# Two-layer cross-attention on one core: the first contexts and queries transposed by TensorE and split from PSUM, key weights' low halves made by GpSimd, TensorE's first work in a fixed order

## The chip, the cores and the metric

One core of a Trainium2 chip. The core has five engines with their own instruction queues: TensorE (PE; its weight loads are listed apart as PEld), VectorE (DVE), ScalarE (ACT), GpSimd (POOL) and SyncE (SP), which here issues nearly all DMAs. Each queue runs in order; engines wait for one another on semaphores. The metric is the device time of one execution in microseconds, the median of several runs.

## The reference, cut to what matters

Two cross-attention layers in float32, batch 8, 100 query rows and 722 context rows of width 512. Layer 0 normalises queries and context with the same gain and bias, has 16 heads of 32, and is followed by a feed-forward block of width 2048; layer 1 attends to the raw context with 16 heads of 64.

```python
qn = _layer_norm(query, ln1_g, ln1_b)
kn = _layer_norm(key, ln1_g, ln1_b)
vn = _layer_norm(value, ln1_g, ln1_b)
Q = (qn @ wq + bq).reshape(B, Sq, H, HD)
K = (kn @ wk + bk).reshape(B, Sk, H, HD)
V = (vn @ wv + bv).reshape(B, Sk, H, HD)
scores = jnp.einsum('bqhd,bkhd->bhqk', Q, K) / jnp.sqrt(jnp.float32(HD))
attn = jax.nn.softmax(scores, axis=-1)
out = jnp.einsum('bhqk,bkhd->bqhd', attn, V).reshape(B, Sq, E)
out = out @ wo + bo
x = residual + out
y = _layer_norm(x, ln2_g, ln2_b)
y = jax.nn.gelu(y @ w1 + b1, approximate=False)
y = y @ w2 + b2
```

## The kernel before, in words

All large products are made in float16 with each operand split in two halves: the high half is the value rounded to float16, the low half what the rounding left. A product is three terms (`TERMS`, line 23): high by high, high by low weight, low by high weight. Weights are scaled by a power of two first, and the layer-0 gain is folded into the weights, its bias into a bias column per output (`bias_mm`, lines 261 to 267: matmuls of the raw float32 weights with one column, 4 per group of 128 outputs).

The program runs through 24 units: 8 of layer 0 (one per batch element, 16 heads each) and 16 of layer 1 (half of the heads of one batch element each). While one unit's heads are worked through, the projections of the next unit, weight preparation and feed-forward pieces are put between the heads; from line 1368 on a scheduler decides the order within each engine by its own estimate of times. Tiles come from pools with a fixed number of buffers, and an instruction waits for the buffer that it needs.

Lines 1257 to 1367 are the opening, in which no attention can run yet. There the kernel lists engines in `nc.in_order`; for those the order of the program text is kept. Before the change these are DVE, ACT, POOL and SP, but not PE.

The opening does this. The eight first inputs are loaded (`first_load`): six chunks of up to 128 rows of context 0 and the queries of batch elements 0 and 1. Each gets statistics (`first_stats`, `first_aggr`) and is normalised in place on DVE (`first_apply`). `first_high` rounds it to float16 on ACT, `first_low` makes the low half on GpSimd and sends both through a DMA transpose, issued by SP, into `ctxT[0, 0]` or `xT[0]`, where the contraction index lies on the partitions. The chunks go in two groups: 0 to 2, then 3 to 7.

Beside this each of the weights wk, wq and wv goes through a fixed series: load (`load0`), sum of squares on ACT (`square_of`), a column sum on PE and a short chain on DVE that gives the scale (`scale_steps`), high halves on ACT (`high0`), low halves on DVE (`low0`, lines 330 to 334), and the bias columns (`bias_mm`, `bias_of`). `biasp` has one PSUM tile for each name: those of k and q from the pool `ps_s` that later holds the scores, that of v from `ps_o`.

Then the first keys are projected: `k0[:2]` are the two halves (361 of 722 columns each) of the first 128 key outputs. Each half is one call of `piece` in `proj_k` (lines 645 to 666): 12 matmuls, the eviction on ACT and DVE to `KN`, and after the second half a store to DRAM (`KD`) and three loads back (`ks`), which put four heads in their place. `first_queries` does the same for the queries through `QD` and `QS`. The first scores (`S`) need both. `load0("o", wo)` and three small columns are loaded after the first group of context 1 has been prepared (`prep0(1)`, lines 1362 to 1367); `wo_block` works on them during the first heads.

Of the kernel before, what the change touches and what calls it, by code (L numbers as in the profile page):

```python
# [54 lines left out]
def xattn_kernel(  # L55
# [38 lines left out]
    def clear_padding0():  # L94
        for t in NM:
            nc.gpsimd.memset(t, 0.0)
        for t in PT:
            nc.gpsimd.memset(t[:, :, SQ:128], 0.0)
        for t in KSR:
            nc.gpsimd.memset(t[:, :, SK:], 0.0)  # L100
            nc.sync.dma_start(out=t[96:98, :, :SK], in_=MSD.rearrange("p (a b) -> p a b", a=4)[:, :, :SK])
# [23 lines left out]
    def psum(shape=(128, 512)):  # L125
        mis["n"] += 1
        if mis["pp"] and mis["n"] % 3 == 0:
            return NZB
        return ps_p.tile(list(shape), F32, tag="pp", name="pp")
# [123 lines left out]
    def load0(name, w, parts=1):  # L253
        raw0[name] = sp.tile([128, KC, E], F32, tag="raw", name=f"raw_{name}", bufs=3)
        for k in range(parts):
            sl = slice(KC // parts * k, KC // parts * (k + 1))
            nc.sync.dma_start(out=raw0[name][:, sl], in_=w.rearrange("(c p) n -> p c n", p=128)[:, sl])
# [1 line left out]
    biasp = {}  # L259

    def bias_mm(name, *ocs):
        if name not in biasp:
            if name == "v":
                biasp[name] = ps_o.tile([128, 512], F32, tag="O", name="bv")[:, :KC]
            else:
                biasp[name] = ps_s.tile([128, 2, 512], F32, tag="S", name="bS")[:, 0, :KC]
        bias_part(biasp[name], raw0[name], b1lc, ocs)

    def bias_of(name, bc, a=0, e=KC):
# [33 lines left out]
    def square_of(name):  # L303
        u = squares[name]
        for k in range(2 if name == "k" else 1):
            sl = slice(2 * k, 2 * k + 2) if name == "k" else slice(0, KC)
            nc.scalar.activation(
                WRES[name][:, 0, sl].rearrange("p c n -> p (c n)"), raw0[name][:, sl].rearrange("p c n -> p (c n)"),
                AF.Square, scale=gbm, accum_out=u[:, 5 * k : 5 * k + 1])
# [3 lines left out]
    def scale_steps(i, name):  # L313

        us = colsum(squares[name], 6)
        ut = small(1, tag="us")
        s = scale0[name] = const.tile([128, 1], F32, name=f"s_{name}")
        gs = gains[name] = const.tile([128, KC], F32, name=f"g_{name}")
        l = [lambda: nc.vector.tensor_reduce(ut, us, AX.X, ALU.add)] + pow2_steps(s, inv0[:, i : i + 1], ut, 0, 1)
        l.insert(5, lambda: nc.vector.tensor_scalar(gs, g1c, s, 1.0 / XS, ALU.mult, ALU.mult))  # L320
        return l
# [3 lines left out]
    def high0(name):  # L325
        w = w0[name] = WRES[name]
        for kc in range(KC):
            nc.scalar.activation(w[:, 0, kc, :], raw0[name][:, kc, :], AF.Copy, scale=gains[name][:, kc : kc + 1])

    def low0(name):  # L330
        w = w0[name]
        for kc in range(KC):
            nc.vector.scalar_tensor_tensor(
                w[:, 1, kc, :], raw0[name][:, kc, :], gains[name][:, kc : kc + 1], w[:, 0, kc, :], ALU.mult, ALU.subtract)

    def split_piece(dst_hi, dst_lo, raw, s, on_pool=False):
        nc.scalar.activation(dst_hi, raw, AF.Copy, scale=s)
# [35 lines left out]
    def hlt():  # L373
        return ring("hl", HL)
# [78 lines left out]
    def first_aggr(c):  # L453
        n = first_in[c][1]
        nc.vector.bn_aggr(mv8[:n, c, :], sts[c][:n])
# [2 lines left out]
        t, n = first_in[c]  # L458
        eng.tensor_scalar(t[:n], t[:n], mv8[:n, c, 0:1], r[:n], ALU.subtract, ALU.mult)

    hls = {}

    def first_high(c, eng):
        t, n = first_in[c]
        h = hls[c] = WRES["v", 0].rearrange("p t (a c) n -> p (t a) (c n)", a=2)[:, c] if c < 4 else hlt()
        (eng.copy if eng is nc.scalar else eng.tensor_copy)(h[:n, :E], t[:n])

    def first_low(c, eng):
        t, n = first_in[c]
        h = hls[c]  # L470
        eng.tensor_tensor(h[:n, E:], t[:n], h[:n, :E], ALU.subtract)
        if c < NCH:
            m = (n + 15) // 16 * 16
            to = ctxT[0, 0][:, :, c * 128 : c * 128 + m]
        else:
            m, to = SQP, xT[0][:, :, (c - NCH) * SQP : (c - NCH + 1) * SQP]
        nc.sync.dma_start_transpose(to, h[:m])

    def first_ucol():
        m2 = small(6, tag="m2")  # L480
# [159 lines left out]

    def proj_k(u):
        L, b, hf = unit_of(u)
        kn = {}

        def piece(oc, j):
            w = w0["k"] if L == 0 else w1res["k", hf]
            T = ctxT[L, b]
            if j == 0:
                kn[oc] = pool.tile([128, 2, SK], F16, tag="KN", name="KN", bufs=2)
            K = kn[oc]  # L650
            ps = psum()
            sl = slice(j * HALF, (j + 1) * HALF)
            for i, (a, w_) in enumerate(TERMS):
                for kc in range(KC):
                    nc.tensor.matmul(
                        out=ps[:, :HALF], lhsT=w[:, w_, kc, oc * 128 : (oc + 1) * 128], rhs=T[:, a * KC + kc, sl],
                        start=(i == 0 and kc == 0), stop=(i == 2 and kc == KC - 1))
            if L == 0:
                bias = bscaled["k"][:, oc : oc + 1]
                nc.scalar.activation(K[:, 0, sl], ps[:, :HALF], AF.Identity, bias=bias)  # L660
                nc.vector.scalar_tensor_tensor(K[:, 1, sl], ps[:, :HALF], bias, K[:, 0, sl], ALU.add, ALU.subtract)
            else:
                nc.scalar.copy(K[:, 0, sl], ps[:, :HALF])
                nc.vector.tensor_tensor(K[:, 1, sl], ps[:, :HALF], K[:, 0, sl], ALU.subtract)
            if j == 1:
                stack(oc)

        def stack(oc):
            K = kn[oc]
            if L == 0:  # L670
                KSt[u, oc] = KS = keys_tile(u, 4 * oc + 3)
                KD = dram.tile([128, 2, SK], F16, tag="KD", name="KD", bufs=4)
                nc.sync.dma_start(out=KD, in_=K)
                src = KD.rearrange("(h d) t k -> d h t k", d=32)
                for r in range(3):
                    nc.sync.dma_start(out=KS[32 * r : 32 * r + 32, :, :SK], in_=src[:, :, r % 2, :])
            else:
                if oc % 2 == 0:
                    KSt[u, oc // 2] = keys_tile(u, 2 * oc + 3)
                KS = KSt[u, oc // 2]  # L680
                for j in range(2):
                    for t in range(2):
                        nc.sync.dma_start(
                            out=KS[64 * t : 64 * t + 64, 2 * (oc % 2) + j, :SK], in_=K[64 * j : 64 * j + 64, t, :])
            if u > 0 and oc == (1 if u == LAST else 2 if u < B else 3):
                load_q(u)
        def item(oc, j):
            f = lambda: piece(oc, j)
            if j == 1 and (L == 0 or oc % 2 == 0):
                f.ready = keys_free  # L690
            return 2.0, f
        return [item(oc, j) for oc in range(4) for j in range(2)]
# [574 lines left out]
    def calls(l):  # L1267
        for f in l:
            f()
# [27 lines left out]
    square_bias("k", bkc)  # L1297
    zip_(A[:6], G_[5:])
    square_of("k")
    bias_mm("k", 0)  # L1300
    K = scale_steps(1, "k")
    calls(A[6:])
    for c in range(3):
        first_apply(c, ra[:, c : c + 1], V)
    for c in range(3):
        first_high(c, S_)
    clear_padding0()
    for c in range(3):
        first_low(c, P_)
    calls(K)  # L1310
    bias_mm("k", 1, 2, 3)
    high0("k")
    load0("v", wv)
    load_early(1, range(4))
    first_stats(3)
# [8 lines left out]
    first_stats(7)  # L1324
    first_aggr(6)
    first_aggr(7)
    Q = scale_steps(0, "q")
    bias_mm("q", 0)
    zip_(Bs, [none] * 3 + Q)
    for c in range(3, 6):  # L1330
        first_apply(c, rb[:, c - 3 : c - 2], V)
        first_high(c, S_)
        first_low(c, P_)
    high0("q")
    for c in range(6, 8):
        first_apply(c, rb[:, c - 3 : c - 2], V)
        first_high(c, S_)
        first_low(c, P_)
    low0("k")
    bias_of("k", bkc)  # L1340
    run(k0[:1])
    low0("q")
    square_bias("v", bvc)
    square_of("v")
    nc.vector.tensor_tensor(sig0, inv0[:, 0:1], inv0[:, 1:2], ALU.mult)
    nc.vector.tensor_scalar(sig0, sig0, 32.0 ** -0.5 * XS / XSQ, None, ALU.mult)
    bias_mm("q", 1)
    bias_of("q", bqc, 0, 2)
    run(k0[1:2])
    first_queries(0)  # L1350
    vs = scale_steps(2, "v")
    bias_mm("q", 2, 3)
    calls(vs)
    high0("v")
    low0("v")
    first_ucol()
    bias_of("q", bqc, 2, 4)
    bias_mm("v", 0, 1, 2, 3)
    nc.in_order = ("sync",)
    bias_of("v", bvc)  # L1360
    nc.in_order = ("vector", "sync")
# [194 lines left out]
```

## Time and profile before

| | us |
|---|---|
| median of 3 runs | 1536.39 (1535.56 to 1539.84) |
| the profiled execution, its time | 1540.27 |
| its span, first to last instruction | 1538.5 |
| busy: PE, DVE, ACT, POOL | 1385.8, 1015.8, 813.6, 580.4 |
| mean granted TensorE clock | 0.966 |

Layer 0 fills the program to about 650 us, layer 1 the rest. A row of the timeline has the start, the length from the first to the last of the merged instructions, the engine, a source line, the operation, output <- inputs, and the number of instructions; in brackets stands the idle time before and what ended it. All instructions pass through one helper, so the source line is 40 for nearly all, and the tiles' names tell them apart: `bS` and `bv` are bias columns, `nzb` the small sums, `pp` the projections. A float32 matmul shows as two rows. The time of a granted clock below 1.00 in a stage is the throttle's, not the kernel's choice.

### The profile page before, as it was taken

What the parts mean: (1) busy time and instruction counts of PE and PEld (TensorE: products, weight loads), DVE (VectorE), ACT (ScalarE), POOL (GpSimd) and SP (SyncE); (2) the same over time, 40 slices, a digit from 0 to 9 for tenths busy, and PEclk for the clock granted to TensorE, in tenths of its full rate; (3) what the DMA queues carried; (4) which work ended last, traced back from release to release, by engine and by line L of the source; (5) the groups of instructions that cost most, each with busy time, mean ns of one, the idle gap of its engine ahead of it and who ended that gap; (6) DMA issues with size and microseconds to landing.
All of it is one profiled execution on the core that took longest, in us unless ns stands there. A gap on an engine that the chain in (4) does not pass through costs nothing. (4 is left out here: it accounts for less than half of the span.)

```text
span 1538.5 us, 33710 instructions
## 1 busy us (share of the span) xinstructions
PE 1385.8 (90%) x12586; PEld 985.0 (64%) x12586; DVE 1015.8 (66%) x2744; ACT 813.6 (53%) x1552; POOL 580.4 (38%) x572
## 2 busy tenths in 40 slices
PE   6888888897878999898999898999899999999996
PEld 5666666676657775566666566666566676566674
DVE  7787888888895676675456755556854555545555
ACT  4455767788865776654354343444343444334442
POOL 4145565665674453452123232122322222323341
PEclk9899999899979999999999999999999999999998
DMA  8567899998966565579577879687768867867684
GB/s 214 131 144 189 211 240 220 238 235 223 239 153 175 164 195 185 132 173 195 144 174 198 173 173 212 160 181 188 176 156 206 187 162 189 185 158 152 149 170 111
DMA packets 456660, 279.20 MB, mean 181 GB/s; under 512 B 348932, under 2 KB 387892, under 8 KB 456496
## 3 DMA queue, kind: packets, MB, share of 16 engines
q1 hardware_dynamic: 454352, 277.02, 74.3%
q8 instruction: 99, 1.62, 0.4%
q14 instruction: 65, 0.53, 0.1%
q10 hardware_dynamic: 2112, 0.01, 0.1%
q0 software_dynamic: 32, 0.01, 0.0%
HBM read 150.88 MB, written 35.30 MB: 121 GB/s over the span
## 5 line engine op out<-in xcount | busy, mean ns | idle before, releaser
L40 POOL TENSOR_TENSOR stage<-p,stage 100x722 f16<-100x722 f32 x124 | 194.1, 1570 | 477.1 <-DVE stage L40 242.3
L40 PE MATMUL pp<-wres,ctxT 128*128 128x256 f16 (+3 forms) x2004 | 335.3, 320 | 8.7 <-DVE KN L40 5.4
L40 PE MATMUL pp<-ctxT,wres 128*128 128x361 f16 x1836 | 326.2, 327 | 17.0 <-DVE V L40 6.3
L40 PEld LDWEIGHTS <-wres 128*128 128x128 f16 x2496 | 240.4, 100 | 144.3 <-issue 22.0
L40 PEld LDWEIGHTS <-ctxT 128*128 128x128 f16 (+1 forms) x2376 | 238.4, 103 | 141.7 <-issue 15.4
L40 DVE TENSOR_REDUCE nm<-S 100x1 f32<-100x722 f32 x256 | 229.9, 900 | 62.0 <-PE S L40 60.3
L40 POOL TENSOR_TENSOR pt<-p,pt 128x300 f16<-128x300 f32 x256 | 200.0, 804 | 180.2 <-ACT pt L40 100.1
L40 PE MATMUL O<-V,pt 128*128 128x64 f16 (+5 forms) x3840 | 201.5, 191 | 27.1 <-DMA pt<-stage 8.2
L40 PEld LDWEIGHTS <-pt 128*128 128x128 f16 (+1 forms) x3840 | 173.7, 99 | 69.2 <-issue 10.2
L40 PE MATMUL S<-ks,QS 128*100 128x361 f16 (+1 forms) x768 | 175.3, 327 | 26.1 <-DVE nm L40 10.8
L40 ACT ACTIVATE p<-S,nb,sig 100x722 f32<-100x722 f32 x128 | 121.8, 953 | 116.3 <-DVE nb L40 99.0
L40 DVE TENSOR_TENSOR V<-pp,V 128x256 f16<-128x256 f32 (+2 forms) x196 | 90.6, 463 | 106.9 <-ACT V L40 106.6
L40 ACT CAST V<-pp 128x256 f16<-128x256 f32 (+2 forms) x196 | 79.2, 407 | 152.7 <-PE pp L40 97.0
L40 PEld LDWEIGHTS <-QS 128*100 128x100 f16 (+1 forms) x768 | 88.5, 127 | 49.4 <-issue 23.6
L40 PEld LDWEIGHTS <-wst 128*128 128x128 f16 x1152 | 100.2, 99 | 13.8 <-DMA wst<-W1S 2.8
L40 ACT ACTIVATE p<-ST,sig 128x600 f32<-128x600 f32 x128 | 97.1, 758 | 13.8 <-PE ST L40 10.0
L40 ACT CAST KN<-pp 128x361 f16<-128x361 f32 x89 | 40.9, 460 | 104.1 <-PE pp L40 92.0
L40 ACT CAST pt<-p 128x600 f16<-128x600 f32 x128 | 88.1, 689 | 2.1
L40 DVE TENSOR_TENSOR KN<-pp,KN 128x361 f16<-128x361 f32 x89 | 47.2, 531 | 56.3 <-ACT KN L40 54.8
L40 PE MATMUL nzb<-ctxT,wres 128*128 128x361 f16 x468 | 81.7, 318 | 2.1 <-DVE sx L40 1.3
L40 PE MATMUL nzb<-wres,ctxT 128*128 128x512 f16 (+2 forms) x372 | 80.6, 366 | 0.2 <-DVE KN L40 0.2
L40 PE MATMUL ST<-QS,ks 98*128 98x100 f16 x768 | 61.0, 212 | 14.7 <-ACT p L40 9.5
(266 smaller groups left out, 2038.9 us busy)
## 6 DMA issues: line engine op xcount, KB each, us to landing
ks<-KN SPq DMA_DIRECT2D x256, 90.2 KB
nat<-in_ctx_dram SPq DMA_DIRECT2D x78, 256.0 KB
ks<-KD SPq DMA_DIRECT2D x96, 180.5 KB
wst<-W1S SPq DMA_DIRECT2D x64, 256.0 KB
wst<-W2S SPq DMA_DIRECT2D x64, 256.0 KB
wst<-WFS SPq DMA_DIRECT2D x48, 256.0 KB
KD<-KN SPq DMA_DIRECT2D x32, 361.0 KB
QS<-QD SPq DMA_DIRECT2D x85, 100.0 KB
```

The source lines that it names most:

```text
L40: r = f(*args, **kwargs)
```

## The change

Eight things, all in the opening:

- The eight DMA transposes go. `first_turn` transposes each normalised chunk in float32 with four TensorE instructions into a half of a PSUM tile of the pool `ps_s`; `first_high` (ACT) and `first_low` (DVE) split from PSUM straight into `ctxT` and `xT`.
- The low halves of the key weights are made by `low0_pool`: ACT scales the raw weights in place, GpSimd subtracts.
- The bias columns of k, q and v share one PSUM tile of `ps_o`.
- TensorE joins `nc.in_order`, so that its work in the opening is done as written.
- `piece` can be called for the matmuls alone, for some of the three terms, or for the eviction alone. The first half of the keys is projected in three steps with other work between.
- The bias columns of q are made one at a time between other work, that of v after the first queries.
- The eviction of the second key half stands between the low halves of the query weights.
- The load of wv and the early loads of context 1 have no DMA transpose ahead of them in SP's queue.

```diff
     def bias_mm(name, *ocs):
-        if name not in biasp:
-            if name == "v":
-                biasp[name] = ps_o.tile([128, 512], F32, tag="O", name="bv")[:, :KC]
-            else:
-                biasp[name] = ps_s.tile([128, 2, 512], F32, tag="S", name="bS")[:, 0, :KC]
+        if not biasp:
+            t = ps_o.tile([128, 512], F32, tag="O", name="bv")
+            for i, k in enumerate("kqv"):
+                biasp[k] = t[:, KC * i : KC * i + KC]
         bias_part(biasp[name], raw0[name], b1lc, ocs)
...
+    def low0_pool(name):
         w = w0[name]
         for kc in range(KC):
...
+            r = raw0[name][:, kc, :]
+            nc.scalar.activation(r, r, AF.Copy, scale=gains[name][:, kc : kc + 1])
+            nc.gpsimd.tensor_tensor(w[:, 1, kc, :], r, w[:, 0, kc, :], ALU.subtract)
...
+    def first_turn(c):
+        t, n = first_in[c]
+        if c % 2 == 0:
+            first_bank[c // 2] = ps_s.tile([128, 2, 512], F32, tag="S", name="T0")
+        ps = first_ps[c] = first_bank[c // 2][:, c % 2].rearrange("p (k n) -> p k n", k=KC)[:, :, :n]
+        for k in range(KC):
+            nc.tensor.transpose(ps[:, k], t[:n, k * 128 : (k + 1) * 128], ident[:n, :n])
+
+    def first_high(c):
+        nc.scalar.copy(first_to(c)[:, :KC], first_ps[c])
+
+    def first_low(c):
+        to = first_to(c)
+        nc.vector.tensor_tensor(to[:, KC:], first_ps[c], to[:, :KC], ALU.subtract)
...
+        def piece(oc, j, part=("mm", "evict"), terms=(0, 1, 2)):
...
+    nc.in_order = ("vector", "scalar", "gpsimd", "sync", "tensor")
     bias_mm("k", 0)
-    K = scale_steps(1, "k")
     calls(A[6:])
     for c in range(3):
         first_apply(c, ra[:, c : c + 1], V)
-    for c in range(3):
-        first_high(c, S_)
-    clear_padding0()
-    for c in range(3):
-        first_low(c, P_)
+        first_turn(c)
+        first_high(c)
+    K = scale_steps(1, "k")
     calls(K)
     bias_mm("k", 1, 2, 3)
     high0("k")
+    for c in range(3):
+        first_low(c)
+    bias_of("k", bkc)
+    clear_padding0()
+    low0_pool("k")
+    half0, half1 = k0[0][1], k0[1][1]
+    half0(("mm",), (0, 1))
     load0("v", wv)
     load_early(1, range(4))
...
+    bias_mm("q", 0)
     Q = scale_steps(0, "q")
-    bias_mm("q", 0)
+    half0(("mm",), (2,))
+    bias_mm("q", 1)
     zip_(Bs, [none] * 3 + Q)
+    half0(("evict",))
+    for c in range(3, 8):
+        first_apply(c, rb[:, c - 3 : c - 2], V)
+        first_turn(c)
+        if c > 3:
+            first_high(c - 1)
     for c in range(3, 6):
-        first_apply(c, rb[:, c - 3 : c - 2], V)
-        first_high(c, S_)
-        first_low(c, P_)
+        first_low(c)
+    bias_mm("q", 2)
+    half1(("mm",))
+    first_high(7)
     high0("q")
     for c in range(6, 8):
-        first_apply(c, rb[:, c - 3 : c - 2], V)
-        first_high(c, S_)
-        first_low(c, P_)
-    low0("k")
-    bias_of("k", bkc)
-    run(k0[:1])
-    low0("q")
+        first_low(c)
+    low0("q", 0, 2)
+    half1(("evict",))
+    low0("q", 2, 4)
     square_bias("v", bvc)
     square_of("v")
+    bias_of("q", bqc, 0, 2)
...
-    bias_mm("q", 1)
-    bias_of("q", bqc, 0, 2)
-    run(k0[1:2])
     first_queries(0)
     vs = scale_steps(2, "v")
-    bias_mm("q", 2, 3)
     calls(vs)
+    bias_mm("v", 0, 1, 2, 3)
     high0("v")
     low0("v")
+    bias_mm("q", 3)
     first_ucol()
     bias_of("q", bqc, 2, 4)
-    bias_mm("v", 0, 1, 2, 3)
```

## The prediction

> **What bounds the kernel now.** I read the page first (PE busy 90% of 1538.5 us), then the first 100 us stage by stage, since the change edits only the opening of the program, then the timeline there engine by engine. The stages (us; busy time and count of PE, PEld, DVE, ACT, POOL; granted clock; DMA share; GB/s):
>
> ```profile
> 0.00:43.00 43.00, 27.92 (x130) 23.51 (x130) 31.16 (x113) 18.74 (x29) 17.46 (x33) 1.00 0.83 197
> 43.00:53.00 10.00, 8.38 (x50) 5.86 (x51) 9.38 (x35) 4.80 (x8) 4.04 (x3) 0.66 0.55 130
> 53.00:66.00 13.00, 7.82 (x64) 5.66 (x62) 8.13 (x20) 6.39 (x16) 1.53 (x2) 0.96 0.83 190
> 66.00:75.00 9.00, 8.83 (x68) 7.43 (x68) 6.05 (x23) 2.66 (x7) 0.95 (x2) 0.68 0.36 99
> ```
>
> Until 43 us nothing is full: the opening is a chain of short waits. From 53 to 66 TensorE idles 5.2 of 13 us, so a front that ends early does not by itself end the program early. TensorE's own rows of the opening (start, length, count):
>
> ```profile
> 9.62 5.71 PE L40 MATMUL bS<-b1lc,raw_k 128*128 128x1 f32 x26 [0.71 <-DMA raw_k<-in_L_xattn_wk_dram]
> 22.17 1.36 PE L40 MATMUL pp<-ctxT,wres 128*128 128x361 f16 x4 [2.34 <-DMA ctxT<-wres]
> 23.33 0.43 PE L40 MATMUL nzb<-u,ones 128*128 128x6 f32 x2
> 25.44 6.99 PE L40 MATMUL bv<-b1lc,raw_v 128*128 128x1 f32 x32 [1.68 <-DMA raw_v<-in_L_xattn_wv_dram]
> 37.06 3.78 PE L40 MATMUL pp<-ctxT,wres 128*128 128x361 f16 x12 [2.20 <-DMA ctxT<-hl]
> 40.99 1.19 PE L40 MATMUL pp<-xT,wres 128*128 128x200 f16 x12 [0.15 <-DVE ra L40]
> 56.76 2.01 PE L40 MATMUL pp<-ctxT,wres 128*128 128x361 f16 x12
> ```
>
> Two things: both halves of the first keys waited for a DMA transpose (2.34 and 2.20 us), which the change removes; and the same twelve key matmuls take 3.78 us at 37 but 2.01 at 56.8. TensorE runs at about half rate through the whole opening although it is given work from 9.6 on, mostly bias columns (0.22 us a row here, 0.12 at 42.2).
>
> What the opening leads to, and what follows it:
>
> ```profile
> 42.10 0.33 SPq L40 DMA_DIRECT2D KD<-KN  x1
> 44.70 1.29 SPq L40 DMA_DIRECT2D ks<-KD  x3
> 46.09 0.64 SPq L40 DMA_DIRECT2D QD<-QN  x1
> 49.44 1.26 SPq L40 DMA_DIRECT2D QS<-QD  x3
> 52.97 0.47 PE L40 MATMUL S<-ks,QS 96*100 96x361 f16 x2
> 54.84 0.54 SPq L40 DMA_DIRECT2D raw_o<-in_L_xattn_wo_dram  x1
> 56.55 0.74 SPq L40 DMA_DIRECT2D b1c<-in_L_xattn_b_dram  x1
> 60.70 0.48 DVE L40 TENSOR_SCALAR acc<-raw_o,bias_v 128x512 f32<-128x512 f32 x1 [2.77 <-DMA raw_o<-in_L_xattn_wo_dram]
> 63.30 0.17 DVE L40 TENSOR_TENSOR bsq<-b1c 128x16 f32<-128x16 f32 x1 [1.99 <-DMA b1c<-in_L_xattn_b_dram]
> ```
>
> From the store of the first keys (KD) to the first score matmul it is 10.87 us of DMA round trips, whatever the engines do. Then DVE stands for two more loads (4.8 us), and TensorE with it. These two waits decide what the front's time is worth.
>
> **The change, part by part.** Durations for the new work, from the rows where the same operations are done later for layer 1 (and GpSimd's subtraction):
>
> ```profile
> L40 PE MATMUL pp<-ident,nat 128*128 128x128 f32 x116 | 18.1, 277 | 0.3 <-DVE V L40 0.3
> L40 ACT ACTIVATE ctxT<-pp,sc 128x512 f16<-128x512 f32 x29 | 19.9, 687 | 15.0 <-PE pp L40 14.4
> L40 DVE SCALAR_TENSOR_TENSOR ctxT<-pp,sc,ctxT 128x512 f16<-128x512 f32 x29 | 21.6, 745 | 8.6 <-ACT ctxT L40 8.4
> L40 POOL TENSOR_TENSOR hl<-nat,hl 128x512 f16<-128x512 f32 x35 | 42.4, 1231 | 28.5 <-ACT hl L40 27.8 <-PE O L40 0.3
> ```
>
> (1) Chunks 0 to 2 through TensorE. A transpose costs 18.1/116 = 0.156 us in a warm stage; scaled by the bias rows' 0.22 against 0.12 it is 0.28 cold. These are its two bounds; the opening is slow, so I take 0.25. The normalised chunks are ready at 11.2, 11.7 and 12.2 (DVE 10.69, 1.46 for three), so twelve transposes run 11.3 to 14.3, and the column sum of the key weights (0.57) ends at 14.9 instead of 15.75: the key scale and the high halves are 0.9 us early (16.2 to 18.75). Key bias columns 1 to 3, formerly ahead of that sum, now follow: 24 rows x 0.22 = 5.2, to 20.1. There the first key matmul starts, 2.1 us before 22.17.
>
> (2) Low halves of the key weights by GpSimd. Four ScalarE scalings in place (0.65 each) may overwrite raw_k only once the bias columns have read it, from 18.8; four subtractions at 1.2 follow, to 24.3, so the second key term ends at 24.6. In the trace DVE made these halves at 29.03 to 31.75. Beside DVE's own SBUF work one such subtraction took 4.44 us here at 29 us, which would add 3.2; now DVE has statistics and PSUM operands beside it, so I take 1.2 and keep 4.44 as the upper bound.
>
> (3) TensorE's order is fixed, and the query column sum now stands behind the GpSimd-paced term and a bias column (8 rows, 1.75): it ends at 26.9 instead of 23.76. On it hangs DVE's interleaved chain (23.80 to 25.9, 2.1 us), then one key eviction (0.6) and five applications (0.49 each): 32.1. In the trace they ended at 29.11. That is the stall that replaces the DMA transposes.
>
> (4) Chunks 3 to 7: twenty transposes at 0.25, from 30.1 to 35.1, a query bias column to 36.8, then the second key half, 3.78 cold, to 40.6; in the trace it ended at 40.84. Evictions 0.56 and 0.60: the store of the first keys goes out at 41.8 instead of 42.10. **Gain 0.3 us, not the 4.5 of the two removed DMA waits.** The queries end by 44.8, hidden under the 46.09 - 42.10 = 4.0 us until SP takes their store. First scores: 41.8 + 10.87 = 52.7 instead of 52.97. SP's queue loses eight transposes and gains nothing in their place; none of them is on this path any more.
>
> (5) Two things are moved past the key store. The value bias (32 rows), done at 25.4 to 32.4 in idle time, now stands at 44.2 with the last query column: 40 rows x 0.12 = 4.8, to 49.0 (0.22: 53.0). And in the built order the first scores stand behind 3 value matmuls, where they stood behind 36: TensorE waits for QS from 49.5 to 52.7 with 33 value matmuls queued behind, 33 x 3.40/23 = 4.9 us of late work. The idle 5.2 us of 53 to 66 covers it; without that cover it costs 4.9.
>
> (6) DVE's preparation of context 1 moves from before to behind the first scores' maximum: that maximum 0.9, statistics, the 2.4 us reciprocal root and three applications end near 58; then ScalarE, three GpSimd subtractions (3.7) and SP's three transposes, and only behind those in SP's queue the load of raw_o, near 64 instead of 54.84. raw_o lands 5.86 later (69.9), b1c 8.46 later (72.4). DVE stops at b1c as before; its first value split behind it comes at 72.4 + 2.5 = 74.9 instead of 72.05, 2.9 late. But both key evictions now stand ahead of that stop, and TensorE has meanwhile done one more value group of 24 (2.78 us in the trace, from 72.02). Net at 75 us: +2.9 - 2.8 = **+0.1 us**.
>
> (7) From there to the middle of the program the built orders differ in their interleaving, without a pattern; after that they are the same. From 100 to 600 us TensorE is busy 432 of 500, 68 us idle; a tenth of that is 7 us, my estimate for either sign, centred on nothing.
>
> The profiled run took 1540.27 us (span 1538.5); plus 0.1 it is 1540.4, and against the median, 3.9 below that run, 1536.5. I round to **1537**.
>
> The Trainium skill has a rule against the change: "TensorE: Matmul & The Clock Gate", Part 4, says that transposes on TensorE do not count as activity for its clock. By it, 32 transposes would not shorten the second key half from 3.78 to 2.01; without it, step 4 would gain up to 1.8 us. The trace agrees as far as it goes, in that bias columns did not speed TensorE up either. The same page's table ("Why this matters for your kernels") warns of idle gaps above about 3 us, after which matmuls are slow again; the 3.2 us of step 5 is such a gap, and by the rule the late value work would cost 0.22 a matmul (the 4.85 us for 22 at 66.17) instead of 0.148.
>
> **Rivals.** *Warm opening (faster).* If the denser order has TensorE at full rate from about 14 us, transposes cost 0.156 (32 x 0.094 = 3.0 saved, all on the chain), key bias 2.9 instead of 5.2 and the two query columns 2.0 less; less what DVE and ScalarE hide of it the store goes out at 36.5, 5.6 early, and QS with it: 1536.4 - 5.6 = 1531. For it: bias rows at 0.12 at 42.2. Against it: 10 us of bias work from 9.6 stayed at 0.22.
>
> *Late value work (slower).* The wait for QS, then DVE's for b1c, take the place of the DMA transposes, and nothing catches up: 2.9 us at DVE, without the credit for the extra group since its evictions pile up on DVE, plus 41 value matmuls at 0.22 instead of 0.148, 3.0 us: 1536.4 + 5.9 = 1542. For it: DVE is 22.25 of 25.00 busy from 75 to 100, so it can't make up much. Against it: TensorE's 5.2 idle us before 66. It decides if raw_o is issued after 64 and TensorE is still behind at 75.
>
> *Reshuffle.* The opening cancels, and the new interleaving up to 600 us costs or gains more than 0.3%: 1536.4 +/- 7, 1529 or 1543.
>
> That the DMA transposes stay can be excluded: they are gone from SP's order.
>
> **How the numbers follow.** Cancelling 0.40; warm 0.18; late value work 0.22; reshuffle 0.10 each way. What a measurement of this kernel can tell from no change is about 0.3%, 4.6 us (its three times span 4.3). Faster 0.18 + 0.10 = 0.28; same 0.40; slower 0.22 + 0.10 = 0.32. The range reaches over both rivals and most of a reshuffle on top of them: 1526 to 1548; the likeliest case alone, 1532 to 1541.
>
> **What would show it.** Right: KD issued at 41 to 42.5, applications of chunks 3 to 7 ending near 32, TensorE waiting about 3 us for QS, raw_o issued near 64, the same order of lengths from 600 us on. Wrong: the second key half in 2.0 instead of 3.8 us, KD before 39 (warm opening); GpSimd's key subtractions far above 1.2; TensorE still waiting on DVE at 80 (late value work).

## The result and the profile after

The change makes the kernel slower: median 1544.53 us (1535.99 to 1557.72, 20 runs) against 1535.97 for the kernel before, run beside it. The ratio is 1.0058 with a 95% interval of 1.0041 to 1.0076, 8.6 us. The profiled execution took 1543.64 us (span 1541.9, mean granted clock 0.961).

The stages of the opening, from the table of windows (us; busy time and count of PE, PEld, DVE, ACT, POOL; granted clock; DMA share; GB/s):

```profile
0.00:43.00 43.00, 29.16 (x134) 23.71 (x134) 29.59 (x107) 21.08 (x33) 9.58 (x29) 1.00 0.54 159
43.00:53.00 10.00, 10.00 (x49) 9.37 (x49) 6.46 (x22) 2.69 (x5) 0.00 (x0) 0.50 0.33 74
53.00:66.00 13.00, 12.24 (x89) 9.06 (x88) 10.91 (x38) 5.41 (x10) 4.89 (x5) 0.86 0.30 57
66.00:75.00 9.00, 6.67 (x70) 5.85 (x68) 3.81 (x11) 4.65 (x12) 0.00 (x0) 1.00 0.98 226
```

From 43 to 53 us TensorE is busy without a pause, at a granted clock of 0.50, while ScalarE and GpSimd have little to do (2.69 and 0.00 us where they had 4.80 and 4.04). A full TensorE with idle neighbours is here the sign of work in the wrong place. From 53 to 66 TensorE fills its old idle time (12.24 us where it had 7.82).

The clock column needs care. It reads 1.00 from 0 to 43 us, though rows there run at half rate (3.78 us for the twelve key matmuls at 35.67, 2.01 at full clock): the trace's first clock record stands at 39.6 us (41.0 in the kernel before), and the column takes 1.00 for the time ahead of it. Nor is a clock below 1.00 only the throttle's affair: the order of the kernel's work moves it, as the end of the experiments shows.

The rows of the opening, from the timeline of the changed kernel, by start:

```profile
20.02 4.50 POOL L40 TENSOR_TENSOR wres<-raw_k,wres 128x512 f16<-128x512 f32 x4 [14.29 <-ACT raw_k L40]
35.67 3.78 PE L40 MATMUL pp<-ctxT,wres 128*128 128x361 f16 x12
40.70 0.33 SPq L40 DMA_DIRECT2D KD<-KN  x1
42.66 6.66 PE L40 MATMUL bv<-b1lc,raw_v 128*128 128x1 f32 x32
49.19 1.84 PE L40 MATMUL bv<-b1lc,raw_q 128*128 128x1 f32 x8
50.90 0.80 PE L40 MATMUL pp<-wres,ctxT 128*128 128x256 f16 x3
51.07 0.16 DVE L40 TENSOR_TENSOR bias_q<-bv,bqc 128x2 f32<-128x2 f32 x1 [2.34 <-PE bv L40]
51.15 0.15 DVE L40 TENSOR_TENSOR bias_v<-bv,bvc 128x4 f32<-128x4 f32 x1
51.22 0.68 DVE L40 BATCH_NORM_STATS2 st<-nat 128x6 f32<-128x512 f32 x1
51.49 0.81 PE L40 MATMUL S<-ks,QS 96*100 96x361 f16 x2
60.94 4.11 SPq L40 DMA_TRANSPOSE ctxT<-hl  x3
65.14 0.54 SPq L40 DMA_DIRECT2D raw_o<-in_L_xattn_wo_dram  x1
72.44 0.18 DVE L40 TENSOR_TENSOR bsq<-b1c 128x16 f32<-128x16 f32 x1 [0.74 <-DMA b1c<-in_L_xattn_b_dram]
74.68 0.41 DVE L40 TENSOR_TENSOR V<-pp,V 128x256 f16<-128x256 f32 x1
77.54 2.74 PE L40 MATMUL pp<-wres,ctxT 128*128 128x256 f16 x12 [2.18 <-DVE V L40]
```

What the change was made for works: the keys are stored at 40.70 instead of 42.10, the first scores come at 51.49 instead of 52.97. The loss stands beside it. The value bias holds TensorE from 42.66; the value projection starts at 50.90. In the timeline of the kernel before, the same projection and the transposes of context 1:

```profile
45.07 3.71 PE L40 MATMUL pp<-wres,ctxT 128*128 128x256 f16 x14 [0.96 <-ACT wres L40]
50.74 4.01 SPq L40 DMA_TRANSPOSE ctxT<-hl  x3
```

The three rows at 51 show a second effect. DVE stands 2.34 us for the last bias column, then adds up `bias_v`, and only then takes the first chunk of context 1. Its order is fixed (`nc.in_order`): the preparation of context 1 is chained behind the sum that reads the value bias. Before, that bias was done at 32.4 and context 1 was normalised from 47.19; now this happens at 58.44. So SP's DMA transposes of context 1 go out at 60.94 instead of 50.74, and `raw_o` behind them at 65.14 instead of 54.84.

The third context is late in its turn. In the timeline of the changed kernel at 110 us, and of the kernel before at the same point of its work:

```profile
118.30 0.69 DVE L40 BATCH_NORM_STATS2 st<-nat 128x6 f32<-128x512 f32 x1 [6.38 <-DMA nat<-in_ctx_dram]
119.36 3.78 PE L40 MATMUL pp<-ctxT,wres 128*128 128x361 f16 x12 [5.73 <-DVE V L40]
```

```profile
107.97 1.28 DVE L40 BATCH_NORM_STATS2 st<-nat 128x6 f32<-128x512 f32 x2 [3.71 <-DMA nat<-in_ctx_dram]
110.79 2.01 PE L40 MATMUL pp<-ctxT,wres 128*128 128x361 f16 x12 [1.87 <-DVE V L40]
```

DVE stands for the next chunk 6.38 us where it stood 3.71, TensorE behind it 5.73 where it stood 1.87, and TensorE then starts slowly: 3.78 us instead of 2.01 for the same twelve matmuls. The loads that DVE stands for are issued at 114.51, behind three DMA transposes at 110.22.

### The profile page after: what moved, and what is told of

Read it like the earlier page. It is cut to its first block, busy times and chain, and to the rows that moved or that the text cites. A ratio compares the mean times of both kernels' runs of the same rounds, so it can differ in the third digit from the quotient of the medians.

```text
span 1541.9 us, 33768 instructions
## 1 busy us (share of the span) xinstructions
PE 1395.7 (91%) x12618; PEld 993.7 (64%) x12618; DVE 1008.7 (65%) x2748; ACT 818.1 (53%) x1556; POOL 573.1 (37%) x568
## 5 line engine op out<-in xcount | busy, mean ns | idle before, releaser
L40 POOL TENSOR_TENSOR pt<-p,pt 128x300 f16<-128x300 f32 x256 | 205.1, 823 | 174.1 <-ACT pt L40 90.2
L40 ACT ACTIVATE p<-ST,sig 128x600 f32<-128x600 f32 x128 | 97.3, 760 | 14.3 <-PE ST L40 8.9
L40 POOL TENSOR_TENSOR hl<-nat,hl 128x512 f16<-128x512 f32 (+2 forms) x48 | 55.5, 1173 | 60.6 <-ACT hl L40 48.7
```

The costliest lines, as they stand in the source:

```text
L40: r = f(*args, **kwargs)
```

## The experiments

Heads are counted from 0, and a head's date is that of ScalarE's exponential. Three theories. **Queue**: the loss comes from the moved bias columns, by way of the value projection and the chain on DVE. **Replan** (Reshuffle in the first expectations): the opening cancels, and the scheduler's new interleaving of layer 0 makes the loss by chance. **Carried**, formed after the bias had been put behind: the late third context at 113 to 119 us is where it is made. Times are given as the ratio to the kernel before run beside it on the same chip, with the 95% interval. Traces of different runs can come from different chips; the kernel before had medians of 1530 to 1539 us on them, so a date of one trace against another is good to a few us.

**Second context freed on DVE** (the changed kernel; the chain on DVE is cut, the value bias stays).

```diff
-    nc.in_order = ("vector", "sync")
+    nc.in_order = ("sync",)
     run(prep0(1)[:1])
+    nc.in_order = ("vector", "sync")
```

> The changed kernel, in which DVE's statistics and normalisation of the second context no longer have to stand behind the value-bias sum in DVE's order; nothing else is edited, though the planner orders the rest anew. Theory Queue (the loss is made before 95 us: the value bias was moved to 42.7-49.2 us on TensorE, its one reader on DVE heads the chain of the second context's preparation, and so SP's transposes, raw_o and b1c come 10 us late, DVE stops at 72 us and the first heads end 5 us late): SP's three transposes issue before 56 us (60.94 in the changed kernel, 50.74 before), raw_o before 60 (65.14, 54.84), head 4's exponential is at most 2.5 us behind the kernel before (5.0 in the changed kernel), and the time is 1.000 to 1.003 of before. Theory Reshuffle (the opening cancels; the new interleaving of layer 0 makes the loss between 100 and 650 us, as in the 5.73 us for which TensorE stands at 113.6): head 4 may come early, but the time stays scattered, 0.997 to 1.009, with no relation to it.

1.0062 (1.0047 to 1.0077). The transposes went out at 49.84 and `raw_o` at 54.05, as Queue said, but head 4 was 9.3 us late and the time did not move. With context 1 out of the way the scheduler put the sum over `raw_o` ahead of DVE's first value evictions, and the stall came back at another place. In its timeline:

```profile
59.99 0.49 DVE L40 TENSOR_SCALAR acc<-raw_o,bias_v 128x512 f32<-128x512 f32 x1 [5.36 <-DMA raw_o<-in_L_xattn_wo_dram]
66.62 2.16 PE L40 MATMUL pp<-xT,wres 128*128 128x200 f16 x12 [5.79 <-DVE V L40]
```

Queue's time (up to 1.003) failed with its head 4. So this run doesn't tell the theories apart; it does show that freeing context 1 alone buys nothing.

**Late loads kept late** (the changed kernel; DVE's and ACT's work on `raw_o`, `g2c`, `b2lc` and `b1c` keeps its place in the text).

```diff
                 if h == 4:
+                    nc.in_order = ("vector", "scalar")
                     wo_block()
+                    nc.in_order = ()
...
+            nc.in_order = ("vector",)
             nc.vector.tensor_tensor(bb, b1c, b1c, ALU.mult)
+            nc.in_order = ()
```

> The changed kernel, in which DVE's and ScalarE's work on raw_o, g2c, b2lc and b1c stands in their queues where the program names it and not as early as the planner likes; the opening up to 66 us is untouched. Theory Queue: DVE no longer stops at 71 to 72.4 us for raw_o and b1c, TensorE's waits for DVE's value evictions at 75 and 77.5 us (1.72 and 2.18 us) shrink by half or more, head 4 is at most 3 us behind the kernel before, time 0.999 to 1.004 of before. Theory Reshuffle: these waits go, but the time lies anywhere from 0.997 to 1.009.

1.0073 (1.0058 to 1.0088). Head 4 was 2.65 us late instead of 5.0, as expected, but the time did not follow: DVE now stood 5.54 us at 72.8 for the next chunk of context 1, and TensorE 5.18 us at 100.9 for `ks`. TensorE's two waits at 75 us became 1.95 and 0.78, not half. Queue's expectation failed: DVE's stop at 72 us alone is not what the change costs.

**The bias moved, alone** (the kernel before with one part of the change: value bias and last query column pinned behind the first queries).

```diff
-    bias_mm("q", 2, 3)
+    bias_mm("q", 2)
     calls(vs)
+    nc.in_order = ("vector", "scalar", "gpsimd", "sync", "tensor")
+    bias_mm("v", 0, 1, 2, 3)
     high0("v")
     low0("v")
+    bias_mm("q", 3)
     first_ucol()
     bias_of("q", bqc, 2, 4)
-    bias_mm("v", 0, 1, 2, 3)
```

> The kernel before with one part of the change alone: the value bias and the last query bias column are pinned on TensorE behind the first queries, as in the changed kernel; DMA transposes, DVE's low halves and all else stay. Theory Queue: the value bias runs at 42 to 50 us instead of 25.4, the second context's three transposes issue at 58 us or later (50.74), raw_o at 62 or later (54.84), head 4 comes 3 to 6 us late, time 1.002 to 1.006 of before. Theory Reshuffle: head 4 is late, yet time 0.997 to 1.009 without relation to it. A theory Transposes (the loss comes from TensorE's 32 added transposes and GpSimd's low halves, none of which are here): 0.999 to 1.001.

1.0117 (1.0100 to 1.0134), from four runs. Head 4 came 5.9 us late. In its timeline the same three signs as in the changed kernel:

```profile
43.66 6.05 PE L40 MATMUL bv<-b1lc,raw_v 128*128 128x1 f32 x32
49.75 0.16 DVE L40 TENSOR_TENSOR bias_v<-bv,bvc 128x4 f32<-128x4 f32 x1 [2.05 <-PE bv L40]
62.18 0.54 SPq L40 DMA_DIRECT2D raw_o<-in_L_xattn_wo_dram  x1
```

This one part, without any TensorE transpose or GpSimd low half, costs more than the whole change, and the theory Transposes (at most 1.001) falls. The size is above Queue's 1.002 to 1.006 and Replan's 1.009, and why it exceeds the change's own is not settled.

**A new plan of the same kernel** (the kernel before; the priority lead of a head's step 103, then 101, in place of 105), to see what a new interleaving does by itself.

```diff
-        with tc.high_priority(offset=80 if u == LAST or u is None and len(pending) and pending[0][0] >= LAST - 1 else 105):
+        with tc.high_priority(offset=80 if u == LAST or u is None and len(pending) and pending[0][0] >= LAST - 1 else 103):
```

> The kernel before with nothing changed but the planner's priority lead of a head's step, 103 in place of 105: a measure of what a new interleaving alone does. Theory Queue: head 4 within 1.5 us of before, and the time within 0.2%, 0.998 to 1.002. Theory Reshuffle: a difference of 0.3% or more to either side.

> The kernel before with the planner's lead at 101: the base of a second pair. Both theories: within 1% of before; Replan expects it slower by 0.2 to 0.6%, like 103, Queue has nothing to say on it.

With 103: 1.0031 (1.0010 to 1.0052). With 101: 1.0054 (1.0034 to 1.0074). Both are slower, although TensorE's rows from 42 to 60 us start within 0.3 us of those of the kernel before. Queue's 1.002 for 103 failed, Replan's two expectations came true: a new interleaving alone is worth up to 0.5%, as much as the change.

**The same for the changed kernel**, which gives two more pairs.

> The changed kernel with the planner's lead of a head's step at 103 in place of 105, the pair of the run of the kernel before with 103 (1.0031). Theory Queue: the pair differs as the two kernels do, 1.007 to 1.011 of before here. Theory Replan: the two kernels with 103 are alike within 0.25%, 1.001 to 1.0055.

> The changed kernel with the lead at 101. Theory Queue: 0.4 to 0.8% above the kernel before with 101. Theory Replan: within 0.25% of it, or scattered to either side.

With 103: 1.0085 (1.0061 to 1.0110), 0.54% above its pair (which ran on another chip), as Queue expected and Replan did not. With 101: 1.0045 (1.0018 to 1.0071), 0.09% below its pair, as Replan expected and Queue did not. In each pair the changed kernel's head 4 comes 4.6 to 7.0 us later, so the damage of the opening is there each time; two interleavings keep it and the third makes it good. The mean over three pairs (0.58, 0.54, -0.09) is 0.34%, 5.3 us, but three values that far apart can't be told from nothing.

**The bias put behind** (the changed kernel; the query column in the gap after the second key half, the value bias after the first third of the value projection, context 1 no longer chained to it).

```diff
     half1(("mm",))
+    bias_mm("q", 3)
...
-    bias_mm("v", 0, 1, 2, 3)
     high0("v")
     low0("v")
-    bias_mm("q", 3)
     first_ucol()
     bias_of("q", bqc, 2, 4)
     nc.in_order = ("sync",)
-    bias_of("v", bvc)
-    nc.in_order = ("vector", "sync")
...
+    first[0] = first[0] + [(1.0, lambda: (bias_mm("v", 0, 1, 2, 3), bias_of("v", bvc)))]
```

> The changed kernel with the two moved pieces of bias work put elsewhere: the last query column behind the second key half (where TensorE stood 1.3 us for DVE), the value bias behind the first third of the value projection and no longer ahead of it; DVE's preparation of the second context no longer stands behind its reader. Theory Queue: the value projection starts near 45.5 us instead of 50.9, the second context's transposes issue by 53 (60.94), raw_o by 57 (65.14), head 4 at most 1 us behind the kernel before (5.0), and the time is 0.997 to 1.001 of before. Theory Replan (any new interleaving of layer 0 costs about what the edited priority alone did, 0.3%, and the opening counts for little): 1.002 to 1.006 although head 4 is on time.

0.9999 (0.9976 to 1.0021): the loss is gone. In its timeline:

```profile
35.26 2.01 PE L40 MATMUL pp<-ctxT,wres 128*128 128x361 f16 x12
45.37 3.70 PE L40 MATMUL pp<-wres,ctxT 128*128 128x256 f16 x14 [2.60 <-ACT wres L40]
52.96 0.54 SPq L40 DMA_DIRECT2D raw_o<-in_L_xattn_wo_dram  x1
```

The value projection starts and `raw_o` is issued where Queue put them. One part of the expectation failed: head 4 was still 5.2 us late and head 8 even 12; head 24 was 0.7 late, head 124 on time. An early head's date tells little about the program's end, since heads and projections share TensorE.

**Loads on a second queue** (the changed kernel; chunks 3 to 5 of contexts 2 to 7 loaded through GpSimd's queue), and **both edits**.

```diff
-                    rows_in(t, cxf, b * SK + c * 128, n, B * SK)
+                    rows_in(t, cxf, b * SK + c * 128, n, B * SK, nc.gpsimd if g == 1 and b > 1 else None)
```

> The changed kernel, in which the loads of chunks 3 to 5 of contexts 2 to 7 are issued by GpSimd's DMA queue, right behind its own work that frees their buffers, and no longer by SP behind three DMA transposes. Theory Carried (the late second context of the opening delays the third one too; its loads are issued at 114.5, DVE stands 6.38 us for them, TensorE 5.73 us, and its next twelve key matmuls take 3.78 us instead of 2.01; that is where the loss is made): DVE's stand for these loads falls below 3 us, TensorE's longest wait between 100 and 125 us below 2.5, and the time is 1.000 to 1.004 of before. Theory Replan: these waits go as well, but the time stays scattered, 0.997 to 1.009.

> Both edits together: the value bias behind the first third of the value projection and the last query column behind the second key half (0.9999 of before by itself), and the loads of chunks 3 to 5 on GpSimd's queue. Theory Carried: little is left for the second edit, since the second context is early here, 0.996 to 1.001. Theory Replan: 0.997 to 1.009.

Alone: 1.0152 (1.0120 to 1.0185), the slowest of all and above both ranges. The stall did shrink, in its timeline:

```profile
121.42 2.00 PE L40 MATMUL pp<-ctxT,wres 128*128 128x361 f16 x12 [3.17 <-DVE KN L40]
```

DVE stood 1.71 us for the load instead of 6.38, and the key matmuls ran at full speed. But DVE then stood 4.30 us at 120.1 for the query rows, so TensorE's longest wait before 125 us was 3.17 and not under 2.5, and TensorE stood 6.56 us at 181.8 behind ScalarE, at two small matmuls that the changed kernel's second profile has at 179.3 without a wait. This stall could be cut and the time grew, so Carried is not supported; since other waits took its place, this run alone doesn't exclude it. With the bias put behind as well: 1.0013 (0.9995 to 1.0032), just above Carried's 1.001, so that edit repairs here too, by 1.4%.

**Both kernels once more**, on one chip.

> The kernel before, once more, on the same chip as the changed kernel in this call: 0.998 to 1.002 of itself. Its trace is for comparison with that one, stage by stage.

> The changed kernel, once more. Both theories: 1.004 to 1.008 of before. Theory Carried: its trace lies level with that of the kernel before up to 100 us within 4 us of TensorE's work, and falls behind by 5 or more between 100 and 125 us. Theory Replan: the loss is made elsewhere on this chip, or in several places.

Before: 1.0017 (0.9993 to 1.0042). After: 1.0059 (1.0036 to 1.0082), 0.42% above it. The loss repeats. The table has all kernels: the date of head 124 of layer 0's 128 in the trace, against the first profile of the kernel before (646.69), and the mean granted clock of all executions (0.967 for the kernel before, run beside them on three chips).

| kernel | head 124, us late | granted clock | ratio of times |
|---|---|---|---|
| bias early or behind: | | | |
| before, again | -2.3 | 0.966 | 1.0017 |
| before, lead 103 | -3.9 | 0.966 | 1.0031 |
| before, lead 101 | +6.6 | 0.966 | 1.0054 |
| changed, bias behind | -0.2 | 0.966 | 0.9999 |
| changed, both edits | +2.4 | 0.966 | 1.0013 |
| bias late: | | | |
| changed, first and again | +8.4, +9.9 | 0.959, 0.959 | 1.0058, 1.0059 |
| before, bias moved alone | +9.3 | 0.961 | 1.0117 |
| changed, second context freed | +4.6 | 0.962 | 1.0062 |
| changed, late loads kept late | -0.4 | 0.965 | 1.0073 |
| changed, lead 103 | +10.1 | 0.958 | 1.0085 |
| changed, lead 101 | +6.0 | 0.965 | 1.0045 |
| changed, second queue | +20.2 | 0.957 | 1.0152 |

From 573 us on the orders of the changed kernel and the kernel before are the same. Head 124 is not where the loss is complete: the changed kernel is 8.4 and 12.2 us behind its neighbour there and 3.4 and 6.1 at the end of these executions. If TensorE's work is counted instead, each kind of row at its median step from one start to the next and bias columns and transposes left out, the second profile of the changed kernel is 0.8 us behind its neighbour at 75 us, 4.0 at 80, 2.8 at 100, 6.4 at 125, 3.6 at 300 and 9.7 at 650. It comes and goes; one stage that owns the loss can't be named. (Carried asked for at most 4 us at 100, which came, and 5 more by 125; it was 3.6.)

What sets the two kernels apart up to head 124 is the clock and not the waits. From the tables of windows, the kernel before and the changed one, from 43 us to head 124:

```profile
43.00:646.69 603.69, 519.61 (x5301) 399.86 (x5302) 466.80 (x1435) 415.75 (x769) 312.39 (x361) 0.93 0.74 194
43.00:655.05 612.05, 530.51 (x5330) 409.56 (x5330) 462.12 (x1444) 417.46 (x770) 312.86 (x361) 0.92 0.73 191
```

TensorE is idle for 84.1 us before and 81.5 after (80.0 and 84.5 in the second profiles); it doesn't wait longer. But its clock, which in these traces is either 0.50 or 1.00, stands at 0.50 for 78.5 us before and 99.0 after (78.5 and 95.6). Twenty us more at half clock are worth up to 10 us, an estimate that takes TensorE as busy all that time. Over all executions the same: a mean clock of 0.959 instead of 0.967 over 1540 us is, by the same estimate, 25 us more at half clock and up to 12 us of time; 8.6 were measured. In the table the clock falls with the late bias, and is back at 0.966 where the bias is put behind; in the changed kernel with lead 101, which lost nothing against its pair, it hardly falls. The two new plans of the kernel before are slower at an unchanged 0.966: that loss is of another kind. The late loads (0.965, yet 1.0073) do not fit. Why a late bias leaves more time at half clock after 75 us is not shown; up to 75 us the two kernels have the same (13.7 us each; 10.2 and 10.3).

## Why the prediction was off

The forecast of 1537 with no change was off by 8 us; its range to 1548 holds the result.

Steps 1 to 3 were right: transposes from 11.32 to 15.1 (14.3 predicted), the first key matmul at 20.25 (20.1), GpSimd's low halves 1.12 each and done at 24.5 (24.3), the query column sum done at 27.0 (26.9). The stall did move from the DMA transposes to that sum: DVE stood 1.44 us for it.

Step 4 had the mechanism and was 1.1 us too cautious: store at 40.70 (41.8), scores at 51.49 (52.7), and the second key half took the 3.78 us assumed; the twenty transposes took 3.9 us and not 5.0. The gain of the front was 1.4 us and not 0.3. This speaks against *Warm opening*.

Step 5 mis-sized a term. The value bias and the query column were put at 0.12 us a row; they took 0.21, 8.4 us and not 4.8 (6.9 in the second profile). So the wait of about 3 us for `QS` did not come (none in the first profile, 1.18 us in the second); TensorE was late instead. (It counted 36 value matmuls ahead of the first scores in the kernel before; the trace has 39.) The cover held: by counted work TensorE was 3.2 and 2.8 us behind at 53 us, and 0.4 and 0.8 at 75.

Step 6 is the one that failed. Its dates were exact (`raw_o` near 64, measured 65.14; `b1c` at 72.4, measured 72.44; the first split at 74.9, measured 74.68), though it missed why: it put context 1 behind the scores' maximum, and the trace has it behind the value bias by the chain on DVE. Its sum for 75 us, +0.1, was nearly met, too (0.4 and 0.8). What failed is closing the sum there. The credit, "- 2.8" for one more value group done, was an advance that the late split took back at once: TensorE stood 1.72 and 2.18 us behind DVE, up to 77.54, and the next 24 value matmuls took 4.25 us where such a group took 2.78 before. At 80 us it was 4.0 us behind in both pairs of profiles, and head 4 came 5.0 us late. The rival *Late value work* (1542) withheld that credit and charged for slow value matmuls. Of its signs `raw_o` after 64 came true; TensorE was hardly behind at 75, and its wait was over before 80.

Step 7 centred the interleaving on nothing. Of the re-planned kernels with the opening of the kernel before, both were slower, by 0.31 and 0.54%. Two such plans are no law, but they speak against a centre of zero; the size of 7 us either way was about right. The rival *Reshuffle* (1543) is as near by its number, but it has the loss made by chance, which the groups below speak against. What step 7 has no term for is the clock: the changed kernel's 17 to 20 us more at half clock between 43 us and head 124.

The cause is shown as far as this: the place of the value bias and the last query column. Moving the two alone into the kernel before costs 1.17%; moving them out of the way gains 0.59% in the changed kernel and 1.39% in the one with the second queue. A new plan by itself is worth up to 0.5%, so one such pair would prove little, but the groups hold together: the seven plans with the two pieces late lie at 1.0045 to 1.0152, 1.0085 in the mean, the five with them elsewhere (the kernel before among them, as 1) at 0.9999 to 1.0054, 1.0019 in the mean. What carries the loss is in the main time at half clock; that is argued from the traces and not tested by an edit. Open are which of the two pieces matters, whether by way of the value projection or of the chain on DVE (cutting the chain alone bought nothing), and what the value bias would cost at its old place ahead of the second key half. No version here beats the kernel before.

The rule drawn on in the prediction (the Trainium skill, "TensorE: Matmul & The Clock Gate", Part 4: transposes do not engage the full clock) agrees with the second key half of 3.78 us in the changed kernel. In the run with the bias put behind it doesn't: the same order of work up to there, and the twelve matmuls took 2.01 us; the clock record has 1.00 from 34.2 us, after 3.4 us of transposes (from 30.76) and nothing else.

## What to carry to other kernels

When an engine's order is fixed, follow each moved instruction to its reader, and the reader's queue to what is chained behind it: here twenty matmuls of one column (40 rows), whose sums nothing read for some 20 us, held back the value projection on one engine and the next context on another. Work that is off the critical path belongs behind the work that others wait for, not at the first place where its data are ready. Compare the granted clock of two kernels and not only their waits. Where a scheduler orders the rest, measure a few new plans of the unchanged kernel before trusting a difference of half a per cent.

## What was not expected of the hardware

Bias columns did not bring TensorE's clock back. In the changed kernel the granted clock fell to 0.50 at 43.0 us and stayed there through 8.0 us in which TensorE did nothing but matmuls of one column, without a pause; it was back at 56.7, 5.8 us after the value matmuls began. In its second profile it was at 0.50 from 44.2 to 54.5, in the kernel before from 44.4 to 51.2 (second profile: 46.4 to 49.8). The Trainium skill, "TensorE: Matmul & The Clock Gate", Part 1, releases the clock after one busy window of about 3.4 us; by that it would have been back by 50 us at the latest, and the trace disagrees for such columns.

The date of the first clock record, with which TensorE reached full speed in the opening, varied with the same order of work: 34.2 us in one run of the changed opening, 38.1 to 38.8 in three, 39.6 to 41.1 in five.
